# A fused deformable-convolution, attention and expert kernel: sums sent by ScalarE, values copied by VectorE, denser side work in the first 26 runs

## The chip, the cores and the metric

The kernel runs on one core of one Trainium2 chip. The metric is the device time of one execution in microseconds (us), the median of three runs.

## The reference

The input `x` has 4 images of 128 channels and 64 x 64 positions. All matrices are float32. Cut to what matters:

```python
# layer 0, for each image
xn  = group_norm(x)                           # 32 groups of 4 channels
om  = conv3x3(xn, w_off and w_mask)           # 18 offsets and 9 masks for every position
smp = bilinear(xn, at 9 taps moved by the offsets) * sigmoid(mask)
x   = x + einsum('bckhw,ock->bohw', smp, w) + bias

# layer 1, for each image: t has 4096 tokens of 128 values
def attn(v):                                  # v = layer_norm(t)
    h  = v.reshape(.., 16 heads, 8) + rx
    c  = cos(h); P = cumprod(c)
    q  = concat(prod(c[1:]), P[1:])           # 8 values per head: queries, keys and values at once
    s  = softmax(q @ q.T / sqrt(8))           # 4096 x 4096 scores per head
    x1 = layer_norm(v + (s @ q) @ w_comb.T)
    f  = relu(cos(x1[:, :8]) * cos(ry) @ w1.T) @ w2.T
    return layer_norm(x1 + f)
t = t + attn(layer_norm(t))
u = layer_norm(t)
p = softmax(u @ router)                       # 8 experts, the two best are taken
t = t + sum over the two best of p_e * (u @ expert_e)
```

## The kernel before, in words

An image is cut into 8 chunks of 512 positions, and its 16 heads into 4 groups of 4. Two kinds of work share the engines.

**Attention steps.** A run is one (image, head group, query chunk), and it goes over key tiles of 128 positions; each key tile is one step, 3700 steps in all. In a step TensorE makes the scores of four heads (`scores`, L1261, four matmuls into two PSUM tiles), ScalarE takes their exponential (L1270, two instructions of 128x1024), and TensorE adds values times exponentials to the run's sum `acc` (`context`, L1281). Scores run two steps ahead of the sums (`LAG`). Some exponentials of later stages are transposed (`turn`, L1140) and used again for the mirrored chunk pair (`from_turned`, L1214).

**Side work.** `prepare(b)` does layer 0 and the queries, keys and values of image `b`. For each chunk `deform` gathers the samples by GpSimd's indirect DMA (L625), weights and adds them on VectorE (L645 to L651), transposes them (L686), and sends them through memory (`smd`, L698 and L731). `convolved` multiplies them with the convolution's weights (`conv_ps`, 18 side products of four matmuls each, L281), adds bias and input on VectorE (L758), and goes on to `features`: layer norm, cosine and the running products `rn` (L822), the copy of `rn` into `fx` with a column of ones (L823, GpSimd), four DMAs of `fx` to `fqd` (L827), the transpose on TensorE (L836), its split into a high and a low part on VectorE (L838, L839), and eight DMAs of these into `kTd` and `qTd` (L846, L847). `finish(b, ch)` does the output projection, the feed-forward part (`feed_forward`) and the experts; up to two finishing jobs are open at once.

**What sets the order.** The order on TensorE, VectorE, SyncE and GpSimd is written out by a planner, class `Beside`. It keeps a clock `now` that moves on by 1.82 us a step, estimated ends of VectorE's and GpSimd's queues, and after each attention step it emits side work that fits. `fills` is how many pieces of side work with TensorE products it may emit in one step, `backlog` how many us of work may already be queued on VectorE. A DMA is put into the queue by `beside.later(when, emit)`, when the planner's clock gets to `when`. Each engine's queue is executed in its order.

**The first runs.** Image 0 has nothing to hide its layer 0 behind, so its attention starts with the chunks that are there. The first 26 runs (`opening`, 160 steps) work on chunks 0 to 3, in pieces; the names are `FIRST` for a run that starts a sum and `MORE` for one that goes on with a sum loaded from memory. Such a run of four steps loads the earlier sum (`cu<-part`, L1456), TensorE adds it through an identity matrix (`acc`, L281), ScalarE copies the total out of PSUM (L1491), and `park_sums` sends it back to memory over SyncE's queue (L1126). In later runs VectorE does the copy and nothing of this is on ScalarE.

The lines of the main loop that the change touches, before:

```python
beside.fills = 3 if run < 12 else 1
if streaming:                      # run < opening
    backlog = 1.5
...
if by_act:                         # run < opening
    nc.scalar.copy(cu, acc)
...
    park_sums(g, sc, cu, beside.now + 3.0 if by_act else beside.dve)
```

Of the kernel before, what the change touches and what calls it, by code (L numbers as in the profile page):

```python
# [22 lines left out]
P = 128  # L23
# [5 lines left out]
CH = 512  # L29
# [3 lines left out]
HD = 8  # L33
NGRP = 4
# [20 lines left out]
QG = 4 * QW  # L55
QL = QG
# [146 lines left out]
def need(pe=0.0, dve=0.0, lat=0.0, hold=False, after=0.0):  # L203

    return pe, dve, lat, hold, after


def ve(n, ops=1):  # L210

    return ops * (0.17 + n / 960.0)
# [6 lines left out]
def tr(n):  # L219

    return 0.13 + 0.115 * n
# [3 lines left out]
def kernel(  # L225
# [22 lines left out]
    nc = tc.nc  # L248
# [12 lines left out]
    beside = Beside()  # L261
# [156 lines left out]
    for i in range(NFX):  # L418
        t = big.tile([P, 4, QR], F32, name=f"fx{i}")
        nc.gpsimd.memset(t, 0.0)  # L420
        h = t[:, :, : HEADS * QW].rearrange("p j (h d) -> p j h d", d=QW)
# [9 lines left out]
    fqd = parked([NGRP, P, 4, QL], "fqd")  # L431
    kTd = parked([P * NGRP, CH], "kTd")
    qTd = parked([P * NGRP, CH], "qTd")
# [3 lines left out]
    partd = [[dram.tile([P, CH], F32, name=f"part{g}_{c}") for c in range(NCH)] for g in range(NGRP)]  # L437
# [355 lines left out]
    def features(b, ch, x2, mean, rstd):  # L793

        yield from layer_norm_stats(x2, mean, rstd, "lt")

        def temp(name, shape=(P, 4 * C), dt=F32):
            return work.tile(list(shape), dt, tag="p2", name=f"{name}{b}_{ch}", bufs=NP2)

        fx, f4 = fxs[ch % NFX]  # L800
        xt, a, n, r = temp("xt"), temp("ra"), temp("rn"), temp("rr")
        yield need(dve=ve(128, 4))
        normalized(xt.rearrange("p (i c) -> p i c", c=C), x2, mean, rstd)
        beside.later(
            beside.dve,
            lambda: nc.sync.dma_start(out=xtd[b][ch].rearrange("p i c -> p (i c)"), in_=xt),
        )
        yield need(dve=ve(512, 2))
        a8 = a.rearrange("p (h d) -> p h d", d=HD)
        x8 = xt.rearrange("p (h d) -> p h d", d=HD)  # L810
        nc.vector.tensor_tensor(a8, x8, rx_sb[:, None, :].to_broadcast([P, 64, HD]), ALU.add)
        yield from cosine(a, a, n, r, ve(512))
        c8 = a.rearrange("p (j h d) -> p j h d", j=4, d=HD)
        q8 = n.rearrange("p (j h d) -> p j h d", j=4, d=HD)
        yield need(dve=ve(64, 7))
        nc.vector.tensor_tensor(q8[:, :, :, 0], c8[:, :, :, 1], c8[:, :, :, 2], ALU.mult)
        for d in range(3, HD):
            nc.vector.tensor_tensor(q8[:, :, :, 0], q8[:, :, :, 0], c8[:, :, :, d], ALU.mult)
        yield need(dve=ve(64, 7), lat=0.2)
        nc.vector.tensor_tensor(q8[:, :, :, 1], c8[:, :, :, 0], c8[:, :, :, 1], ALU.mult)  # L820
        for d in range(2, HD):
            nc.vector.tensor_tensor(q8[:, :, :, d], q8[:, :, :, d - 1], c8[:, :, :, d], ALU.mult)  # L822
        beside.later(beside.dve, lambda: nc.gpsimd.tensor_copy(f4[:, :, :, :HD], q8))  # L823

        def put_values():
            for g in range(NGRP):
                nc.sync.dma_start(out=fqd[b % 2][ch][g], in_=fx[:, :, QG * g : QG * g + QL])  # L827

        beside.later(beside.dve + 2.0, put_values)

        yield need(pe=tr(4), dve=ve(512, 2))
        pt = misc(f"fT_ps{b}_{ch}")
        for i in range(4):
            nc.tensor.transpose(pt[:, P * i : P * (i + 1)], n[:, P * i : P * (i + 1)], ident)  # L836
        hi, lo = temp("hiT"), temp("loT")
        nc.vector.tensor_copy(hi.bitcast(F32R), pt)  # L838
        nc.vector.tensor_tensor(lo.bitcast(F32R), pt, hi, ALU.subtract)  # L839

        def put(part, fT):

            kd = kTd[b % 2][ch].rearrange("(h l r d) n -> l r h d n", l=2, r=2, d=HD)
            qd = qTd[b % 2][ch].rearrange("(h r l d) n -> l r h d n", l=2, r=2, d=HD)
            for rep in range(2):
                nc.sync.dma_start(out=kd[part, rep], in_=fT)  # L846
                nc.sync.dma_start(out=qd[part, rep], in_=fT)  # L847

        beside.later(beside.dve - ve(512), lambda: put(0, hi))
        beside.later(beside.dve, lambda: put(1, lo))  # L850
        prepared[b, ch] = beside.dve + 9.0
        featuring.pop(0)

# [65 lines left out]

    def feed_forward(b, ch, x4, a4):  # L920

        z3 = [
            work.tile([P, 4, HD], F32, tag=f"zf{k}", name=f"zf{k}{b}_{ch}") for k in range(3)
        ]
        zf = z3[0]
        yield need(dve=3 * ve(32))
        nc.vector.tensor_copy(zf, a4[:, :, :HD])
        yield from cosine(zf, *z3, ve(32))

        zx = work.tile([P, 4, 4, HD], F32, tag="zx", name=f"zx{b}_{ch}")  # L930
        yield need(dve=ve(32, 4), lat=0.2)
        nc.vector.tensor_tensor(zf, zf, cry[:, None, :].to_broadcast([P, 4, HD]), ALU.mult)
        nc.vector.tensor_copy(zx[:, :, 0, :].bitcast(F32R), zf)
        nc.vector.tensor_tensor(zx[:, :, 2, :].bitcast(F32R), zf, zx[:, :, 0, :], ALU.subtract)
        nc.vector.tensor_copy(zx[:, :, 1::2, :], zx[:, :, 0::2, :])
        yield need(pe=tr(4), dve=ve(512), lat=0.2)
        pz = misc(f"z_ps{b}_{ch}")
        for i in range(4):
            nc.tensor.transpose(
                pz[:32, P * i : P * (i + 1)], zx[:, i].rearrange("p l d -> p (l d)"), ident  # L940
            )
        zT = work.tile([32, 512], F32R, tag="f2", name=f"zT{b}_{ch}", bufs=NF2)
        nc.vector.tensor_copy(zT, pz[:32, :])
        hT = []
        for f in range(FFN // P):
            yield need(pe=0.43, dve=ve(512), lat=FREE if f < 3 else 0.2)
            ph = misc(f"h_ps{b}_{ch}_{f}")
            nc.tensor.matmul(ph, lhsT=w1_x[:, P * f : P * (f + 1)], rhs=zT, start=True, stop=True)  # L948
            h = temp2(f"h{b}_{ch}_{f}", (P, 512))
            nc.vector.tensor_scalar(h, ph, b1_sb[:, f : f + 1], 0.0, ALU.add, ALU.max)  # L950
            hT.append(h)
        yield need(dve=ve(512))
        nc.vector.tensor_tensor(a4, a4, bc4(b2), ALU.add)
        for i in range(4):
            for f in range(FFN // P):
                if f % 2 == 0:
                    last = i == 3 and f == 2
                    yield need(pe=2 * MM128, dve=ve(512) if last else 0.0, lat=0.0 if last else FREE, hold=not last)
                if i == 0 and f == 0:
                    pf = misc(f"f_ps{b}_{ch}")  # L960
                by_columns(
                    pf[:, C * i : C * (i + 1)], hT[f][:, P * i : P * (i + 1)], w2_sb[:, f, :],
                    f == 0, f == FFN // P - 1,
                )
        nc.vector.tensor_tensor(a4, a4, pf.rearrange("p (i c) -> p i c", c=C), ALU.add)  # L965
        m = work.tile([P, 4], F32, tag="ln_m", name=f"m2{b}_{ch}")
        rs = work.tile([P, 4], F32, tag="ln_r", name=f"r2{b}_{ch}")
        yield from layer_norm_stats(a4, m, rs, "ln")
        yield need(dve=ve(128, 4))
        normalized(a4, a4, m, rs)  # L970
        yield need(dve=ve(512, 2))
        nc.vector.tensor_tensor(a4, a4, bc4(g2), ALU.mult)
        nc.vector.tensor_tensor(a4, a4, bc4(beta2), ALU.add)
        yield need(dve=ve(512))
        nc.vector.tensor_tensor(x4, x4, a4, ALU.add)
# [144 lines left out]

        beside.later(beside.dve, put)

    def park_sums(g, sc, cu, when):

        def put():
            nc.sync.dma_start(out=partd[g][sc], in_=cu)  # L1126
            storing.discard((g, sc))

        storing.add((g, sc))
        beside.later(when, put)  # L1130

# [90 lines left out]

    landing = {}
    fetched = {}
    groups, done, active = {}, [], []

    def finishing():

# [179 lines left out]
    with tc.manual_schedule(engines={PE, DVE, SP, POOL}):  # L1410
# [6 lines left out]
        while n < len(steps):  # L1417
# [17 lines left out]
                    gives.remove(steps[m])  # L1435
                    turn(es[m - n], *steps[m])

            beside.fills = 3 if run < 12 else 1
            if streaming:
                backlog = 1.5  # L1440
            else:
                backlog = 0.4 if at >= len(ts) - 3 else 3.2
            if b + 1 < NB:
# [45 lines left out]
                cu = work.tile([P, 512], F32, tag="cu", name=f"cu{run}", bufs=NCU)  # L1489
            if by_act:  # L1490
                nc.scalar.copy(cu, acc)  # L1491
            elif kind in (WHOLE, FIRST):
                nc.vector.tensor_copy(cu, acc)  # L1493
            else:
                nc.vector.tensor_tensor(cu, cu, acc, ALU.add)
            if kind in (WHOLE, LAST):
                park_context(b, g, sc, cu)
            else:
                park_sums(g, sc, cu, beside.now + 3.0 if by_act else beside.dve)
        alone.append(True)  # L1500
        beside.drain()

# [72 lines left out]
```

## Time and profile before

| | |
|---|---|
| median of three runs | 7609.23 us (7607.39 to 7621.65) |
| profiled execution, its own time | 7579.71 us |
| its span, first to last instruction | 7576.5 us |
| mean granted TensorE clock | 0.968 |
| TensorE busy | 7113.9 us, 94% |
| ScalarE busy | 6863.5 us, 91% |
| VectorE busy | 4465.9 us, 59% |
| GpSimd busy | 1653.2 us, 22% |
| first exponential of step 0 | at 176 us |
| first exponential of step 160 (end of the first 26 runs) | at 637 us |
| last step's sums end | at 7493 us |

The share of TensorE is that of pipelined matmuls whose ends are modelled, so it reads high. SyncE and the DMA-issuing parts of the other engines are shown as queues (SPq, ACTq, POOLq): a row there is the time that the engine took to issue a transfer, not the transfer. In a list of waits a row names who waited, for whom, the sum in us, how many times, and the longest.

### The profile page before, as it was taken

The numbers are of one execution on the slowest core, as the hardware profiler recorded it, in microseconds if no ns is written. First come the engines' busy times: TensorE is split into PE (matmuls) and PEld (weight loads), VectorE is DVE, ScalarE is ACT, GpSimd is POOL, SyncE is SP. The second block draws the span as 40 slices with busy tenths as digits, with TensorE's granted clock in tenths as the row PEclk, the third lists the DMA queues.
The fourth block names the chain that finished last, engine by engine and source line by source line (L and its number), as shares of the span: only waits on it lengthen the run. The fifth ranks groups of instructions, "written<-read, shape, count | busy, mean of one in ns | idle before, by whom it ended". The sixth has DMA issues, their size and how long they took to land.

```text
span 7576.5 us, 180754 instructions
## 1 busy us (share of the span) xinstructions
PE 7113.9 (94%) x73848; PEld 2375.9 (31%) x73848; DVE 4465.9 (59%) x8950; ACT 6863.5 (91%) x7467; POOL 1653.2 (22%) x1326
## 2 busy tenths in 40 slices
PE   3688999899999999999999999999999999999997
PEld 2122222223333333333333323333333333333333
DVE  7755356667444877776544677775444554455434
ACT  0578999889999999999999998989999999999995
POOL 5544034443000433422000334431000000000000
PEclk6889999999999999999999999999999999999998
DMA  6777567978446878887655789897454466666661
GB/s 181 223 204 219 141 223 241 300 234 291 149 168 200 292 244 280 268 277 244 203 179 190 228 279 298 289 324 237 174 190 152 148 236 230 232 222 239 226 202 63
DMA packets 909788, 1689.51 MB, mean 223 GB/s; under 512 B 150754, under 2 KB 384124, under 8 KB 858268
## 3 DMA queue, kind: packets, MB, share of 16 engines
q1 hardware_dynamic: 809102, 1371.37, 54.9%
q0 software_dynamic: 92160, 302.06, 12.4%
q8 instruction: 579, 9.49, 0.5%
q10 hardware_dynamic: 7694, 4.52, 0.2%
q14 instruction: 253, 2.07, 0.1%
HBM read 1027.51 MB, written 650.14 MB: 221 GB/s over the span
## 4 chain that ended last, share of the span: by engine, by line
PE 80%; DMA 8%; DVE 4%; issue 2%; ACT 2%; SPq 1%; another core or an unknown queue 0%; POOL 0%; POOLq 0%; DVEq 0%; ACTq 0%
PE acc L1281 39%; PE sc L1261 24%; PE acc L1214 5%; PE e_ps L281 4%; PE conv_ps L281 3%; DMA et<-etd 2%; PE f_ps L281 2%; ACT e L1270 2%; DMA etd<-st 1%; DMA sT<-smd 1%; PE om_ps L533 1%; DMA smd<-tr 1%; DVE st L1140 1%; DVE v L645 1%; DMA cu<-part 1%
## 5 line engine op out<-in xcount | busy, mean ns | idle before, releaser
L1270 ACT ACTIVATE e<-sc 128x1024 f32<-128x1024 f32 x7400 | 6849.4, 1081 | 527.0 <-PE sc L1261 368.1
L1281 PE MATMUL acc<-e,qf 128*9 128x512 f32 (+1 forms) x29600 | 3938.3, 601 | 18.6 <-ACT cu L1491 7.5
L1261 PE MATMUL sc<-qT,kT 32*128 32x512 f32 x14800 | 2368.7, 499 | 153.3 <-ACT e L1270 84.8
L1261 PEld LDWEIGHTS sc<-qT,kT 32*128 32x128 f32 x14800 | 942.8, 183 | 3612.6 <-ACT e L1270 3130.4
L625 POOL DMA_INDIRECT v<-tab,idx x1152 | 1451.8, 1260 | 1579.3 <-DVE tr L686 956.2
L1140 DVE STREAM_TRANSPOSE st<-e 128x1024 f32<-128x1024 f32 x792 | 937.3, 1222 | 752.4 <-ACT e L1270 620.1
L1281 PEld LDWEIGHTS acc<-e,qf 128*9 128x9 f32 (+1 forms) x29600 | 682.4, 91 | 610.3 <-issue 346.8
L396 POOL TENSOR_TENSOR r<-ln_t,expo 128x4 f32<-128x4 f32 x96 | 112.2, 1169 | 3105.4 <-DVE ln_t L394 3057.0
L645 DVE TENSOR_TENSOR v<-v,wt 128x1536 f32<-128x1536 f32 x384 | 667.0, 1737 | 119.5 <-DMA v<-tab,idx 96.8
L1214 PE MATMUL acc<-et,qv 128*9 128x128 f32 x12672 | 506.4, 276 | 52.2 <-DMA et<-etd 44.6
L1065 DVE TENSOR_TENSOR eo<-e_ps,gt 128x512 f32<-128x512 f32 x256 | 175.2, 686 | 552.5 <-PE e_ps L281 547.5
L650 DVE TENSOR_TENSOR v<-v 128x768 f32<-128x768 f32 x384 | 367.2, 956 | 10.1
L281 PE MATMUL conv_ps<-sT,wconv_sb 128*32 128x256 f32 x4320 | 351.0, 399 | 15.7 <-DMA sT<-smd 11.6
L1214 PEld LDWEIGHTS acc<-et,qv 128*9 128x9 f32 x12672 | 270.0, 90 | 254.4 <-issue 212.6
L686 DVE STREAM_TRANSPOSE tr<-v 128x128 f32<-128x128 f32 x1080 | 249.4, 282 | 37.5 <-DMA etd<-st 28.7
L1493 DVE COPY cu<-acc 128x512 f32<-128x512 f32 x116 | 80.2, 692 | 306.3 <-PE acc L1281 260.8
L651 DVE TENSOR_TENSOR v<-v 128x384 f32<-128x384 f32 x384 | 215.7, 562 | 13.3
L396 POOL TENSOR_TENSOR rstd<-lt_t,expo 128x4 f32<-128x4 f32 x32 | 57.9, 1811 | 575.9 <-DVE lt_t L394 550.7
L281 PE MATMUL f_ps<-w_sb,h 128*32 128x128 f32 x4096 | 166.1, 282 | 0.1
L950 DVE TENSOR_SCALAR h<-h_ps,b_sb 128x512 f32<-128x512 f32 x128 | 94.9, 744 | 100.3 <-PE h_ps L948 89.9
L823 POOL COPY fx<-rn 128x512 f32<-128x512 f32 x32 | 26.8, 838 | 526.3 <-DVE rn L822 321.4
L965 DVE TENSOR_TENSOR a<-a,f_ps 128x512 f32<-128x512 f32 x32 | 21.9, 685 | 198.8 <-PE f_ps L281 198.8
(227 smaller groups left out, 3166.9 us busy)
## 6 DMA issues: line engine op xcount, KB each, us to landing
etd<-st SPq DMA_DIRECT2D x396, 1024.0 KB
et<-etd SPq DMA_DIRECT2D x396, 1024.0 KB
kT<-kTd SPq DMA_DIRECT2D x372, 256.0 KB
smd<-tr SPq DMA_DIRECT2D x360, 192.0 KB
sT<-smd SPq DMA_DIRECT2D x360, 192.0 KB
qT<-qTd SPq DMA_DIRECT2D x166, 256.0 KB
atd<-cu SPq DMA_DIRECT2D x128, 256.0 KB
qf<-fqd SPq DMA_DIRECT2D x372, 72.0 KB
```

The lines of the kernel that those rows point to most:

```text
L281: nc.tensor.matmul(dst[c : c + 32], lhsT=lhsT[:, c : c + 32], rhs=rhs, start=start, stop=stop)
L625: nc.gpsimd.indirect_dma_start(out=v[:, k, :], out_offset=None, in_=tab, in_offset=bass.IndirectOffsetOnAxis(ap=idx[:, j, kk : kk + 1], ax ...
L645: nc.vector.tensor_tensor(v4, v4, w12[:, :, None].to_broadcast([P, 12, C]), ALU.mult)
L650: nc.vector.tensor_tensor(v[:, :, : 2 * C], v[:, :, : 2 * C], v[:, :, 2 * C :], ALU.add)
L651: nc.vector.tensor_tensor(v[:, :, :C], v[:, :, :C], v[:, :, C : 2 * C], ALU.add)
L686: nc.vector.transpose(out=tr9[:, k, :, j % 4, :], in_=v[:, k, :C].rearrange("p (c i) -> p c i", i=32),)
L1065: nc.vector.tensor_tensor(ws[hf], pe.rearrange("p (e c) -> p e c", c=C), gt[:, i, 4 * hf : 4 * (hf + 1), None].to_broadcast([P, 4, C]), AL ...
L1140: nc.vector.transpose(out=st[:, :, 2 * pr : 2 * pr + 2, :].rearrange("p o h (q j) -> p o (h q) j", j=32), in_=es[pr].rearrange("p h (q o i ...
L1214: nc.tensor.matmul(acc[32 * h : 32 * h + QW, P * kt : P * (kt + 1)], lhsT=qv[:, at : at + QW], rhs=e[:, :, h, 32 * t : 32 * (t + 1)], star ...
L1261: nc.tensor.matmul(ps[i // 2][:, i % 2, :], lhsT=kT[h : h + 32, P * (t % 4) : P * (t % 4 + 1)], rhs=qT[h : h + 32, :], start=True, stop=True,)
L1270: nc.scalar.activation(e, ps[pr], AF.Exp, scale=1.0 / math.sqrt(HD))
L1281: nc.tensor.matmul(acc[32 * h : 32 * h + width, :], lhsT=flat[:, first : first + width], rhs=es[h // 2][:, h % 2, :], start=(t == ts[0]), ...
```

## The change

It does six things.

1. In the first 26 runs, in place of the first 12, up to three pieces of side work with TensorE products are emitted in a step.
2. In these runs VectorE's queue may hold 4.0 us in place of 1.5 us.
3. In these runs ScalarE issues the store of its sum itself, in its own queue.
4. `rn` is copied into `fx` by VectorE, after the high and the low part, and `fx` is sent by one DMA in place of four, last.
5. `hiT` and `loT` are sent by two DMAs each in place of four; a row of the tile is written twice by a repeated source, and the order of rows within a head becomes (d, part, repeat) in keys and (d, repeat, part) in queries.
6. `feed_forward` waits while another finishing job is inside its feed-forward part (list `heavy`).

```diff
@@ features
-        beside.later(beside.dve, lambda: nc.gpsimd.tensor_copy(f4[:, :, :, :HD], q8))
-        def put_values():
-            for g in range(NGRP):
-                nc.sync.dma_start(out=fqd[b % 2][ch][g], in_=fx[:, :, QG * g : QG * g + QL])
-        beside.later(beside.dve + 2.0, put_values)
-        yield need(pe=tr(4), dve=ve(512, 2))
+        yield need(pe=tr(4), dve=ve(512, 3))
...
         nc.vector.tensor_tensor(lo.bitcast(F32R), pt, hi, ALU.subtract)
+        nc.vector.tensor_copy(f4[:, :, :, :HD], q8)
         def put(part, fT):
-            kd = kTd[b % 2][ch].rearrange("(h l r d) n -> l r h d n", l=2, r=2, d=HD)
-            qd = qTd[b % 2][ch].rearrange("(h r l d) n -> l r h d n", l=2, r=2, d=HD)
-            for rep in range(2):
-                nc.sync.dma_start(out=kd[part, rep], in_=fT)
-                nc.sync.dma_start(out=qd[part, rep], in_=fT)
-        beside.later(beside.dve - ve(512), lambda: put(0, hi))
-        beside.later(beside.dve, lambda: put(1, lo))
+            kd = kTd[b % 2][ch].rearrange("(p l r) n -> l p r n", l=2, r=2)
+            qd = qTd[b % 2][ch].rearrange("(p r l) n -> l p r n", l=2, r=2)
+            twice = fT[:, None, :].to_broadcast([P, 2, CH])
+            nc.sync.dma_start(out=kd[part], in_=twice)
+            nc.sync.dma_start(out=qd[part], in_=twice)
+        def put_values():
+            nc.sync.dma_start(
+                out=fqd[b % 2][ch].rearrange("g p t x -> p t g x"),
+                in_=fx.rearrange("p t (g x) -> p t g x", g=NGRP),
+            )
+        beside.later(beside.dve - 2.0 * ve(512), lambda: put(0, hi))
+        beside.later(beside.dve - ve(512), lambda: put(1, lo))
+        beside.later(beside.dve, put_values)
@@ feed_forward
+        while heavy:
+            yield need(lat=1.0)
+        heavy.append(True)
...
         nc.vector.tensor_tensor(a4, a4, pf.rearrange("p (i c) -> p i c", c=C), ALU.add)
+        heavy.pop()
@@ main loop
-            beside.fills = 3 if run < 12 else 1
+            beside.fills = 3 if streaming else 1
             if streaming:
-                backlog = 1.5
+                backlog = 4.0
...
             if by_act:
                 nc.scalar.copy(cu, acc)
+                nc.scalar.dma_start(out=partd[g][sc], in_=cu)
...
-            else:
-                park_sums(g, sc, cu, beside.now + 3.0 if by_act else beside.dve)
+            elif not by_act:
+                park_sums(g, sc, cu)
```

More of the change, by code (lines that the diff above doesn't have):

```diff
@@ L1121, in park_context, with park_sums @@
         beside.later(beside.dve, put)
-    def park_sums(g, sc, cu, when):
+    def park_sums(g, sc, cu):
         def put():
@@ L1129, in park_sums @@
         storing.add((g, sc))
-        beside.later(when, put)
+        beside.later(beside.dve, put)
     def turn(es, run, t):
@@ L1226 @@
     fetched = {}
-    groups, done, active = {}, [], []
+    groups, done, active, heavy = {}, [], [], []
     def finishing():
```

## The prediction

> **What bounds the kernel now.** I read the page first, then busy time by stage.
>
> ```profile
> PE 7113.9 (94%) x73848; PEld 2375.9 (31%) x73848; DVE 4465.9 (59%) x8950; ACT 6863.5 (91%) x7467; POOL 1653.2 (22%) x1326
> 176.00:640.00 464.00, 349.01 (x2756) 101.16 (x2752) 306.57 (x556) 315.19 (x349) 250.12 (x190) 0.84 0.74 225
> 640.00:1000.00 360.00, 341.78 (x2812) 99.77 (x2812) 154.17 (x304) 335.13 (x364) 69.68 (x56) 0.97 0.52 150
> 1000.00:5300.00 4300.00, 4141.34 (x42659) 1358.67 (x42647) 2780.92 (x5304) 4021.37 (x4360) 1184.61 (x947) 0.98 0.76 247
> 5300.00:7493.00 2193.00, 2190.35 (x24672) 758.23 (x24674) 1049.36 (x2437) 2189.67 (x2394) 52.28 (x51) 1.00 0.58 199
> ```
>
> The columns are length, then busy us of PE, PEld, DVE, ACT, POOL, then granted clock. In the last long stage ScalarE idles 3 us of 2193: its exponentials set the pace: 2394 of them in 2193 us, two a step, so 1.83 us a step. TensorE fits beside them as long as a step carries one side product. So the time is 3700 steps at that pace plus ScalarE's idle time: 176 us ahead of the first step, 149 us in the first 26 runs (176 to 640), 25 us to 1000, 279 us to 5300, and the 84 us tail. Five of the six edits aim at the second term. The gaps there, from ScalarE's timeline:
>
> ```profile
> 267.53 5.61 ACT L1270 ACTIVATE e<-sc 128x1024 f32<-128x1024 f32 x6 [45.60 <-PE sc L1261]
> 286.54 0.59 ACT L1491 COPY cu<-acc 128x512 f32<-128x512 f32 x1 [10.68 <-issue]
> 491.94 5.61 ACT L1270 ACTIVATE e<-sc 128x1024 f32<-128x1024 f32 x6 [14.00 <-PE sc L1261]
> 509.71 0.58 ACT L1491 COPY cu<-acc 128x512 f32<-128x512 f32 x1 [9.43 <-PE acc L281]
> 900.73 3.77 ACT L1270 ACTIVATE e<-sc 128x1024 f32<-128x1024 f32 x4 [10.83 <-PE sc L1261]
> ```
>
> 267 is the wait for chunk 1, 492 for the keys of chunk 3, 900 for those of chunk 7. The gaps before copies (L1491) are runs whose earlier sum came late from memory; those of 0.3 us and more add up to 42 us (10.7, 4.2, 0.3, 2.2, 9.4, 1.8, 2.0, 4.1, 7.4). Then the waits from 0 to 760 us, SyncE's queue among them:
>
> ```profile
> SPq L1126 <- ACT cu L1491: 113.8, 15, 19.9
> SPq L827 <- POOL fx L823: 45.0, 6, 13.4
> DVE xr L758 <- PE conv_ps L281: 88.7, 5, 25.6
> PE sc L1261 <- DMA kT<-kTd: 37.2, 3, 22.0
> ```
>
> SyncE's queue, which carries nearly every transfer, stands 114 us behind stores that wait for ScalarE and 45 us behind GpSimd's copy; VectorE stands 89 us waiting for convolutions that are fed one product a step.
>
> **The change part by part**, against the profiled 7579.7 us (span 7576.5 and 3.2 around it); the median of the runs shown is 7609.2, 29.5 above. Signs: minus is a gain.
>
> *Key and value path (edits 4, 5).* For chunk 0 SyncE issues fqd from 153.26 to 155.86, and the eight stores of high and low parts from 156.41 to 162.81, about 0.6 us each; the loads start at 170.39 when these have landed. With four stores in place of eight, and fqd behind them, the keys' last store goes out up to 4 us earlier. Each new store is twice as big, so its issue may take 0.6 us as now or twice that: the gain is between 0 and 4. I take 4, as the issue of fqd's four quarters shows no growth with more and smaller pieces (0.65 each). For chunk 1 fqd runs from 244.78 and kTd's last from 253.21, with smd's stores behind; four issues less and fqd gone from the front are about 5 us of the 45.6. Together −9 (0 to −14). The copy on VectorE costs 0.43 us (its cheapest 512-wide pass, L373) to 0.69 us (L811), 32 times, 14 to 22 us. I take 0.69, since it writes rows of 9. VectorE is 59% busy and the copy stands behind the high and low parts, so nothing waits for it but fqd: 0; uncovered it costs 22. GpSimd's queue loses 32 copies that stand in front of gathers: from 441.6 to 458.3 no gather was issued, because the copy waited for `rn`.
>
> A rule speaks against this edit. The Trainium skill, SBUF — State Buffer, section SBUF: two separate sides, says that an fp32 copy from SBUF to SBUF on VectorE locks GpSimd out of descriptor generation, so that gathers stall. By that rule the 32 copies would each hold the gathers up for their length, at most 22 us in all, 5.5 us of it in the eight of image 0. In this case's trace the gathers' issues take 0.94 to 2.4 us each beside a busy VectorE, and this spread may hold such holds already; one more pass of 0.69 us in a chunk of 36 gathers and some 75 us of VectorE work is below what I count.
>
> *Three side products a step (edit 1) and the longer queue (2).* The built instruction lists of the changed kernel have the convolution of chunk 3 in steps 68 to 73 in place of 70 to 87, and the transposes L836 of chunks 2 to 7 at steps 45, 88, 126, 165, 230, 278 in place of 47, 100, 136, 186, 237, 282. Chunk 3's keys are first needed at step 104, now 16 steps (29 us) after the transpose and not 4: the wait of 14.0 goes, −14 (what is next there is the sum of the next row). Chunk 7 is needed from step 288 on; 4 steps earlier (7.3 us) and a shorter put take 9 of the 10.8. What it costs is seen where image 0 already ran three a step:
>
> ```profile
> 303.38 1.94 ACT L1270 ACTIVATE e<-sc 128x1024 f32<-128x1024 f32 x2 [0.27 <-PE sc L1261]
> 306.10 1.94 ACT L1270 ACTIVATE e<-sc 128x1024 f32<-128x1024 f32 x2 [0.79 <-PE sc L1261]
> 308.84 1.94 ACT L1270 ACTIVATE e<-sc 128x1024 f32<-128x1024 f32 x2 [0.80 <-PE sc L1261]
> ```
>
> A step with three products takes 2.73 us, one with a single product 1.86 (TensorE's sums at 416.99, 418.86 and 420.72). Three convolutions (chunks 3, 4, 5), 18 triple steps: 18 x 0.87 = 15.7, less the 36 steps that lose their product, 36 x 0.03 = 1.1: +14.6. Where the run waits for its sum anyway it is hidden; bounds +5 and +15, I take +14. The longer queue puts up to 2.5 us more of gathers' sums ahead of a convolution's result on VectorE; behind that wait TensorE's single side bank. I take 0 (−5 to +10).
>
> *Sums by ScalarE (3).* 26 stores leave SyncE. Each costs ScalarE an issue: ACTq rows of like size took 0.36 to 0.44 us, so 26 x 0.40 = 10.4; ScalarE is busy 315 of 464 there, and busier at run ends: +8 (bounds 7 and 11). What SyncE gains is the place of the next loads. A load of a sum still stands behind `sT` and `smd` issues, and behind the store two runs before it, which uses the same buffer. So I take a third of the 42 us, −14 (0 to −42). There is a new wait: in the built lists each DMA of SyncE and ScalarE takes the next of eight completion counters and waits until the previous DMA on that counter has landed. So ScalarE, with all later exponentials queued behind it, waits for a transfer of SyncE eight DMAs back. For 17 of the 26 that was emitted 6 steps or more (11 us) before. Nine are nearer; the worst is the store of run 24, in the same step as a `sT` load. Loads here took 6.5 to 13 us: +8 (0 to +40, if SyncE runs late for a dozen of them).
>
> The Trainium skill, DMA: Bandwidth & Descriptors, section Issuing engines are not separate DMA queues, says that spreading DMAs over issuing engines saves sequencer issue time alone. By that the gain would be 26 x 0.33 = 8.6 us of SPq's issue, and not more; the row of 113.8 us says that the queue's wait is worth more than its issue.
>
> *One job in the feed-forward part (6).* The lists have the same TensorE work left after step 3700, so the tail stays at 84. Jobs interleave otherwise; the side work done by step 2000 is 1% less. Of the 279 us of gaps to 5300, many are `et<-etd` landing late or scores waiting for exponentials, which a new interleaving shifts either way. I take 0, bounds −20 and +20.
>
> Sum: −9 −14 −9 +14 +8 −14 +8 = −16. GpSimd's queue, whose gathers start up to 16 us earlier in a chunk, should now and then free VectorE: −3 (0 to −10). That is −19: 7560.7 for a profiled execution like this one, about 7590 against the median of 7609.2.
>
> **Rivals.** *The queue was the whole trouble.* All waits for sums go, chunk 7's whole wait too, and ScalarE's new wait is nothing: −9 −14 −11 +14 +8 −42 = −54, 7555. For it: 114 us on one row. Against: sums late at 388.79 and 496.30 were issued right behind `sT` loads, which stay.
>
> *ScalarE is tied to SyncE (slower).* ScalarE, the pacing engine, inherits SyncE's lateness through the eight counters. If a dozen stores wait 6.5 us (the landing at 277.61 to 284.5), it is 78 us; with the first sum without its +8 (−24) the result is +54, 7663; with eight such waits +28, 7637. It decides from 24 us on, four such waits. For it: SyncE's stores of `smd` wait for VectorE, whose queue is now longer. Against: the planner's step is 1.82 us and real steps of this stage take 2.9, so SyncE is rather ahead of the list than behind.
>
> *Given back.* The chunks come earlier than any step needs (chunks 4 and 5 are needed at step 256 only), and triple steps cost what the waits gave: 7609.
>
> **How the numbers follow.** Own sum 0.45, whole queue 0.20, tied to SyncE 0.25, given back 0.10. A measurement tells 0.2% (15 us) from no change. My own sum lies just beyond that, its bounds on both sides of it: 0.25 faster, 0.15 same, 0.05 slower. The whole queue is faster, 0.20. Tied: 0.22 slower, 0.03 same. Given back: 0.06 same, 0.04 slower. Total 0.45, 0.24, 0.31. The range from 7540 to 7645 takes in the second rival's time and the first half of the third's; the likeliest case alone, whose bounds are not all met at once, is 7570 to 7615.
>
> **What would show it.** Right: step 160 begins some 20 us earlier than 637; no gap of 14 us at chunk 3; the row SPq for ScalarE's copy gone; triple steps of 2.7 us in runs 13 to 25. Wrong: ScalarE's queue waiting several us before its stores; gaps at copies as long as before; or a difference that arises after 1000 us, where I count nothing.

## The result, and the profile after

The changed kernel takes **7678.2 us** (median of four runs, 7667.1 to 7685.5) against 7608.3 for the kernel before in the same comparison: ratio **1.0089 [1.0068, 1.011]**, some 70 us slower. The forecast was 7590, range 7540 to 7645, most likely a gain. The profiled execution of the changed kernel takes 7684.0 us, 6 above its median; that of before lies 29 under its own. The two traces are therefore 104 us apart, the medians 70, and I use the traces for where the loss arises rather than for its size.

The first line is from the page; the others are busy time by stage, with the columns of the prediction (the stages begin at the same steps as there, to within some us):

```profile
PE 7144.8 (93%) x73848; PEld 2383.3 (31%) x73848; DVE 4473.2 (58%) x8982; ACT 6866.5 (89%) x7467; POOL 1620.4 (21%) x1294
```

```profile
180.00:634.00 454.00, 353.10 (x2808) 104.66 (x2808) 313.49 (x594) 316.10 (x351) 233.82 (x179) 0.87 0.77 227
634.00:1000.00 366.00, 349.33 (x2816) 101.31 (x2820) 147.56 (x275) 341.75 (x371) 71.14 (x58) 0.96 0.53 151
1000.00:5400.00 4400.00, 4154.23 (x42417) 1357.04 (x42411) 2775.72 (x5290) 4010.05 (x4344) 1164.21 (x922) 0.97 0.74 241
5400.00:7600.00 2200.00, 2196.56 (x24859) 762.43 (x24860) 1060.59 (x2475) 2196.31 (x2401) 52.78 (x52) 1.00 0.58 198
```

ScalarE's busy time is what it was; its idle time grew. It idles 138 us in the first stage (149 before) and 390 us in the third, which is 4400 us long (279 in 4300 before). The fourth is still limited by the exponentials, with 4 us idle. The start of a step's first exponential in both traces says where:

| step | before, us | after, us | difference |
|---|---|---|---|
| 104 | 491.9 | 486.3 | -5.7 |
| 160 | 637.0 | 629.9 | -7.1 |
| 288 | 882.3 | 871.8 | -10.6 |
| 400 | 1108.5 | 1101.8 | -6.7 |
| 800 | 1940.0 | 1957.6 | +17.6 |
| 1200 | 2702.5 | 2732.9 | +30.4 |
| 1720 | 3725.4 | 3793.5 | +68.1 |
| 2500 | 5276.7 | 5383.6 | +106.9 |
| 3699 | 7489.9 | 7596.6 | +106.8 |

The first image gains 11 us. Steps 400 to 2500, in which images 1 to 3 are prepared beside the scores, lose 114 us. After that nothing changes. This is the third of the signs that the prediction named as proof against itself: a difference where it counted nothing.

**The opening.** From ScalarE's timeline (start, duration, operation, idle time ahead of it and what ended it):

```profile
269.92 5.61 ACT L1275 ACTIVATE e<-sc 128x1024 f32<-128x1024 f32 x6 [41.68 <-PE sc L1266]
291.19 0.59 ACT L1496 COPY cu<-acc 128x512 f32<-128x512 f32 x1 [12.93 <-PE acc L281]
490.34 1.23 ACT L1275 ACTIVATE e<-sc 128x1024 f32<-128x1024 f32 x1
490.67 0.33 ACTq L1497 DMA_DIRECT2D part<-cu  x1
498.40 0.59 ACT L1496 COPY cu<-acc 128x512 f32<-128x512 f32 x1 [4.08 <-PE acc L281]
589.63 0.59 ACT L1496 COPY cu<-acc 128x512 f32<-128x512 f32 x1 [14.94 <-PE acc L281]
886.88 1.94 ACT L1275 ACTIVATE e<-sc 128x1024 f32<-128x1024 f32 x2 [7.44 <-PE sc L1266]
```

The 14.0 us wait for chunk 3's keys is gone: around 490 the exponentials run through. Steps 70 to 72, with three products each, take 2.66 to 2.79 us, near the 2.73 forecast; where loads came late, others took up to 4.4. The wait for chunk 7 is 7.4 in place of 10.8. But the gaps ahead of copies, most of which end with a sum's load, are not smaller: all rows with a gap add up to 58 us, to 49 before (the 42 of the prediction leave out four rows of 0.3 us and more). ScalarE's own store (ACTq) starts 0.03 us after the copy's end in 25 of 26 cases, 0.27 in the other: no long wait for a completion counter shows.

The wait for chunk 1 is 4 us shorter only because the first step began 3.7 us later (at 179.9, before at 176.2). From the start of VectorE's pass `hiT`, which makes the chunk's keys, to the first exponential on them it took 20.1 us before (247.46 to 267.53) and takes 24.5 now (245.38 to 269.92). SyncE's queue shows where, first before, then after:

```profile
254.79 4.12 SPq L698 DMA_DIRECT2D smd<-tr  x4
261.00 0.34 SPq L1239 DMA_DIRECT2D kT<-kTd  x1
```

```profile
249.70 1.67 SPq L844 DMA_DIRECT2D fqd<-fx  x1
251.46 11.82 SPq L698 DMA_DIRECT2D smd<-tr  x4
263.78 0.41 SPq L1244 DMA_DIRECT2D kT<-kTd  x1
```

The keys' last store is issued 5 us earlier than before. But the four stores of samples (`smd`) behind the value transfer now take 11.8 us to issue, and the loads of the keys stand behind them.

**The middle.** What TensorE and the scores waited for between 900 and 5400 us (sum in us, times, longest):

```profile
ACT e L1275 <- PE sc L1266: 235.6, 146, 13.0
PE acc L1219 <- DMA et<-etd: 64.8, 20, 10.2
PE conv_ps L281 <- DMA sT<-smd: 41.1, 8, 11.6
```

The same three rows of before read 154.9, 44.6 and 7.8. ScalarE waits 81 us more for scores, and TensorE waits 54 us more for loads: of samples (`sT`) for the convolutions, and of turned exponentials (`et`). Both are issued by SyncE. The granted clock of the third stage is 0.97, before 0.98, and TensorE is busy 4154 us in it, before 4141; whether the lower clock adds to the gaps or follows from them isn't shown.

### The profile page after: what moved, and what is told of

It is laid out like the page before. It is cut to its first block, busy times and chain, and to the rows that moved or that the text cites. A ratio compares the mean times of both kernels' runs of the same rounds, so it can differ in the third digit from the quotient of the medians.

```text
span 7682.2 us, 180344 instructions
## 1 busy us (share of the span) xinstructions
PE 7144.8 (93%) x73848; PEld 2383.3 (31%) x73848; DVE 4473.2 (58%) x8982; ACT 6866.5 (89%) x7467; POOL 1620.4 (21%) x1294
## 4 chain that ended last, share of the span: by engine, by line
PE 81%; DMA 8%; DVE 3%; issue 3%; SPq 2%; ACT 2%; POOL 1%; another core or an unknown queue 0%; ACTq 0%; POOLq 0%; DVEq 0%
PE acc L1286 39%; PE sc L1266 24%; PE acc L1219 5%; PE conv_ps L281 4%; PE e_ps L281 3%; DMA et<-etd 3%; DMA sT<-smd 2%; ACT e L1275 2%; PE f_ps L281 2%; PE om_ps L533 1%; DMA a<-rdd 1%; POOL v L625 1%; SPq L722 1%; PE ao_ps L281 1%
## 5 line engine op out<-in xcount | busy, mean ns | idle before, releaser
L281 PEld LDWEIGHTS conv_ps<-sT,wconv_sb 128*32 128x32 f32 x4320 | 92.1, 110 | 184.6 <-issue 163.3
L758 DVE SCALAR_TENSOR_TENSOR xr<-conv_ps,bconv_sb,xr 128x128 f32<-128x128 f32 x128 | 35.9, 343 | 153.3 <-PE conv_ps L281 144.9
```

The source lines that it names most:

```text
L281: nc.tensor.matmul(dst[c : c + 32], lhsT=lhsT[:, c : c + 32], rhs=rhs, start=start, stop=stop)
```

## The experiments

Each group of runs shares one chip and the runs of the kernel before on it. Chips differ (the unedited kernel takes 7463 to 7614 us), so only ratios and differences within a group are compared; where a trace is laid against that of before across groups, it says so. The planner's step, `STEP`, is a constant of 1.82 us by which it places side work. Another value changes no operation, only the step in which each is emitted; I call that re-dealing.

**Which edit loses? (7611.1 before)** Parts of the change alone, as hunks of the diff above.

```diff
open_only:      edits 1, 2, 3     lock_only:     edit 6
open_and_lock:  edits 1, 2, 3, 6  path_and_lock: edits 4, 5, 6
```

> The kernel before with edits 1, 2 and 3 alone (the first 26 runs); value path and feed-forward part as before. The two traces differ by 11 us in favour of the change up to step 300 and by 118 us against it from step 400 to step 2500, so the loss should not be here. Queue theory (the value path's transfers, edits 4 and 5, block SyncE's queue): 7595, some 11 us faster than before, and no loss after step 400. Lock theory (edit 6 makes the loss): the same 7595. Re-dealing theory (any edit shifts the planner's order in images 1 to 3, and a new order costs tens of us whoever made it): 7590 to 7670, with a loss after step 400, since this edit too shifts the later order.

> The kernel before with edit 6 alone: one finishing job at a time in its feed-forward part. Lock theory: 7670 to 7700, nearly the whole loss, between steps 800 and 2500, where the finishing jobs run. Queue theory: 7600 to 7615, no loss. Re-dealing theory: anywhere from 7580 to 7660.

> The changed kernel without edits 4 and 5: edits 1, 2, 3 and 6, with GpSimd's copy of the values, four value transfers ahead of eight key and query stores. Queue theory: the loss is gone, 7590 to 7605. Lock theory: the loss stays, 7665 to 7690. Re-dealing theory: between the two, with no relation to the sum of the single parts.

> The kernel before with edits 4, 5 and 6, the first 26 runs as before. Queue theory: 7680 to 7700, the whole loss without the gain of the opening, and the transfer that follows the single value transfer takes several us to issue in every chunk, as in the changed kernel. Lock theory: the same time as with the lock alone. Re-dealing theory: anywhere from 7590 to 7690.

Measured: open_only 7606.6, 0.9995 [0.9985, 1.0005]; lock_only 7637.8, 1.004 [1.0025, 1.0054]; open_and_lock 7645.8, 1.0049 [1.0033, 1.0066]; path_and_lock 7665.1, 1.0072 [1.0055, 1.0089]. Laid against the first trace of before (another run, of nearly the same time), step 300 comes 10 us earlier in open_only, and by step 500 the gain is gone. So the opening edits do what the traces of the whole change showed, and give nothing in the end. The lock alone seems to cost 27 us. Without edits 4 and 5 (open_and_lock) half the loss is there, which neither the queue theory nor the lock theory had forecast. Edits 4 and 5 without edit 6 were not tried.

**Is it the lock, the form of the path, or the order? (7578.5 before)** The lock could cost by what it does, or only because any new order does.

```diff
old_path_same_order: changed kernel, with GpSimd's copy, four fqd DMAs
                     ahead of the transpose, eight stores
small_transfers:     changed kernel, with four fqd DMAs last, eight stores
redealt_before:      before, and
-    STEP = 1.82
+    STEP = 1.81
redealt_lock:        before with edit 6, and
-    STEP = 1.82
+    STEP = 1.83
```

> The changed kernel with the old value and key path (GpSimd's copy, four value transfers ahead of eight stores), but with the planner told what it is told in the changed kernel. TensorE and ScalarE execute exactly the changed kernel's order, VectorE too but for the copy; only the transfers' form and place differ. Queue theory: the path's share comes back, 7640 to 7655, since the transfer behind the single value transfer no longer takes 5 us to issue. Re-dealing theory: it stays at 7670 to 7685, since the order is that of the changed kernel.

> The changed kernel with four value transfers and eight stores again in their old forms, but in the changed kernel's places (high, low, values last) and with VectorE's copy. All orders but SyncE's are those of the changed kernel. Queue theory, form: 7640 to 7655, the burst of 256-row transfers is what blocks the queue. Queue theory, place: 7670 to 7685, the same pieces in the same place fill the queue whoever cuts them, and the next transfer still takes several us. Re-dealing theory: 7670 to 7685.

> The kernel before with nothing changed but the planner's idea of a step, 1.81 us in place of 1.82. The work and all mechanisms are the same; the order of side work is dealt anew. Re-dealing theory: the time moves by 20 us or more, up or down. Lock and queue theories: 7600 to 7620, as before.

> The kernel with edit 6 alone (7638 against 7611 in the run before), and the planner's step at 1.83 us in place of 1.82. Lock theory: 7630 to 7650, the lock costs the same in any order. Re-dealing theory: it moves by 15 us or more from 7638, either way.

Measured: old_path_same_order 7657.4, 1.0094 [1.0077, 1.0111]; small_transfers 7678.7, 1.0127 [1.0109, 1.0146]; redealt_before 7602.2, 1.0025 [1.0015, 1.0035]; redealt_lock 7554.1, **0.9953 [0.9935, 0.9972]** (its medians alone give 0.9968). The first of these is the plainest: with the old value and key path back, in the changed kernel's order, the loss is as large as that of the whole change. The queue theory had forecast that some half of it would go, the re-dealing theory that all of it would stay. In the trace of old_path_same_order, steps 300 to 2500 take 4449 us, in that of before (another chip) 4360, in the changed kernel's 4478:

```profile
912.70:5361.70 4449.00, 4218.15 (x43103) 1379.99 (x43104) 2781.91 (x5278) 4082.14 (x4420) 1188.05 (x954) 0.98 0.74 240
```

ScalarE idles 367 us there, before 283. The lock theory falls too: with the lock and a planner step 0.01 us longer the kernel is faster than either version (it has the lowest ratio found). And 0.01 us of planner step alone moves the unedited kernel by 0.25%. Smaller transfers do not help while they stand last, so the size of a single transfer is not the cause.

**How far does re-dealing move the changed kernel? (7602.0 before)**

```diff
changed_again: as changed      changed_183: changed, STEP = 1.83
changed_181: changed, STEP = 1.81
open_and_lock_183: edits 1, 2, 3, 6, STEP = 1.83
```

> The changed kernel itself, so that its re-dealt forms are compared on one chip: 1.009 times before, as found.

> The changed kernel with all six edits and the planner's step at 1.83 us in place of 1.82: same work, same mechanisms, side work dealt anew. Re-dealing theory: it moves by 20 us or more from the changed kernel, and downwards, since the changed kernel's order is the worst of those seen: a ratio to before of 0.995 to 1.006. Queue and lock theories: 1.006 to 1.012, as the changed kernel.

> The same with 1.81 us. Re-dealing theory: a ratio between 0.995 and 1.008, not that of the other two. Queue and lock theories: 1.006 to 1.012.

> Edits 1, 2, 3 and 6 with the planner's step at 1.83 us. The lock with 1.83 gave 0.9953 of before. If the opening's 10 to 15 us came on top: 0.993 to 0.994. Re-dealing theory: the edits of the opening shift the order again, so no such sum holds: 0.994 to 1.006.

Measured: changed_again 7663.7, 1.0078 [1.0061, 1.0095]; changed_183 7661.9, 1.0073 [1.0046, 1.0101]; changed_181 7626.8, 1.0034 [1.0019, 1.0048]; open_and_lock_183 7638.9, 1.0056 [1.0038, 1.0074]. The loss repeats on another chip. Re-dealing takes some 37 us of it away, but none of the three orders tried of the changed kernel gets back to the time before. That points to something besides the order, but three orders do not show it.

**The place of the value transfers (7614.2 before).** The same instruction order on TensorE and ScalarE in both of the first two kernels; the copy is VectorE's and the transfers are the small ones in both. Only the place differs: `fqd` ahead of the transpose, as before the change, or last, behind `loT`.

```diff
 place_values_last = small_transfers; place_values_first:
+        nc.vector.tensor_copy(f4[:, :, :, :HD], q8)
+        def put_values(): ...    # four DMAs
+        beside.later(beside.dve + 2.0, put_values)
         yield need(pe=tr(4), dve=ve(512, 3))
...
-        beside.later(beside.dve, put_values)
 lock_184: edit 6, STEP = 1.84     before_180: before, STEP = 1.80
```

> The changed kernel's order on TensorE, ScalarE and GpSimd, VectorE's copy, four value transfers and eight stores, but the values' copy and transfers ahead of the transpose as in the kernel before. Against the same pieces with the values last (next run): if the place is what costs, some 20 us less, as with the old path; if GpSimd's copy was what helped there, no difference.

> The same pieces with the values last (small_transfers again, as the partner of the run above on one chip). Place: some 20 us above it. No place: equal within 8 us. Either way 1.007 to 1.013 of before.

> Edit 6 alone with the planner's step at 1.84 us. With 1.82 it was 1.004 of before, with 1.83 it was 0.995. If the lock itself costs some 30 us and 1.83 was a lucky order: 1.002 to 1.006. If the order alone decides: anywhere from 0.995 to 1.005.

> The kernel before, without any edit, with the planner's step at 1.80 us. 1.81 gave 1.0025. If orders without the lock are better as a family: 0.998 to 1.003. If the order alone decides: anywhere from 0.995 to 1.006.

Measured: place_values_first 7659.3, 1.0052 [1.0036, 1.0069]; place_values_last 7730.8, 1.0145 [1.0128, 1.0162]. The place alone is worth 72 us, far more than the 20 expected. lock_184 takes 7633.9, 1.0025 [1.0011, 1.0038], which both theories allow. before_180 takes 7672.9, 1.007 [1.0053, 1.0088], above what both allow: a version of the unedited kernel loses nearly as much as the change.

**The same with one transfer (7462.6 before).** The whole change, and the whole change with only its `fqd` DMA and the copy in front of it moved back ahead of the transpose.

```diff
 changed_control: as changed; changed_values_first:
+        nc.vector.tensor_copy(f4[:, :, :, :HD], q8)
+        def put_values(): ...    # the one DMA of the change
+        beside.later(beside.dve + 2.0, put_values)
         yield need(pe=tr(4), dve=ve(512, 3))
...
-        beside.later(beside.dve, put_values)
```

> The changed kernel, transfers in its own forms and VectorE's copy, with the copy and the one value transfer back in their old place, ahead of the transpose and of the eight... now four stores. All other orders are the changed kernel's. If the place costs in this form too: 20 us or more below the changed kernel (next run), 1.003 to 1.006 of before, and the transfer behind the burst no longer takes 5 us to issue. If only the cut into four with values last is bad: equal to the changed kernel, 1.008 to 1.009.

> The changed kernel as it is, on the same chip: 1.008 to 1.009 of before.

Measured: changed_values_first 7457.6, **0.9992 [0.9983, 1.0001]**; changed_control 7523.7, **1.0082 [1.0068, 1.0096]**. That is 66 us, as much as the change had lost on this chip (61). Between the two traces the difference is +1 us at step 300, +25 at 800, +49 at 1720 and +63 from 2500 on. It arises in the same stretch as the loss of the change. Steps 300 to 2500 of each, in the columns used above, control first:

```profile
889.60:5219.80 4330.20, 4136.33 (x43105) 1359.14 (x43107) 2787.44 (x5302) 4070.96 (x4421) 1183.09 (x930) 0.98 0.75 247
```

```profile
888.20:5156.50 4268.30, 4123.51 (x43101) 1357.02 (x43102) 2789.59 (x5304) 4069.66 (x4420) 1182.71 (x930) 0.98 0.76 251
```

The same work, with the clock at 0.98 in both; TensorE is busy 13 us longer in the control. ScalarE idles 259 us in one and 199 in the other, and this is 61 of the 62 us. One of the places, around step 465: first SyncE's queue and TensorE in changed_control,

```profile
1188.66 1.25 SPq L841 DMA_DIRECT2D qTd<-loT  x1
1190.01 1.28 SPq L844 DMA_DIRECT2D fqd<-fx  x1
1191.34 3.17 SPq L1461 DMA_DIRECT2D cu<-part  x1
...
1195.99 8.93 SPq L731 DMA_DIRECT2D sT<-smd  x8
1207.21 0.93 PE L1266 MATMUL sc<-qT,kT 32*128 32x512 f32 x4
1213.09 1.08 PE L281 MATMUL conv_ps<-sT,wconv_sb 128*32 128x256 f32 x8 [4.95 <-DMA sT<-smd]
```

and then the same place in changed_values_first:

```profile
1181.65 0.62 SPq L826 DMA_DIRECT2D fqd<-fx  x1
...
1187.33 1.25 SPq L847 DMA_DIRECT2D qTd<-loT  x1
1188.63 1.31 SPq L1460 DMA_DIRECT2D cu<-part  x1
...
1192.29 4.83 SPq L731 DMA_DIRECT2D sT<-smd  x8
1205.55 0.92 PE L1265 MATMUL sc<-qT,kT 32*128 32x512 f32 x4
1206.40 0.64 PE L281 MATMUL conv_ps<-sT,wconv_sb 128*32 128x256 f32 x8
```

Here the values go out 4 us ahead of the first of the keys' stores (1185.5), in a pause of the queue. In the control they stand between the keys' stores and the next chunk's loads. There the DMA behind them takes 3.17 us to issue in place of 1.31, the eight `sT` loads are issued by 1204.9 in place of 1197.1, and the first convolution of the next chunk waits 4.95 us. TensorE's queue, with all the scores, stands behind it. The five steps from 465 take 15.9 us in the control and 9.4 in the other. At steps 530, 575, 1405 and 2150, too, the control falls behind by 5 to 8 us within ten steps. The longest waits there are 9.5 us for `et` (1405, in the other kernel 2.8) and 13.5 and 9.3 us for `sT` (575 and 2150, in the other 9.0 and 3.7), not all of them directly behind a value transfer. From 900 to 5250 us TensorE's waits for `sT` add up to 47.1 us against 25.8, those for `et` to 91.8 against 76.9: 36 of the 62 us are on these two rows.

**Five forms in one order.** These kernels have the same order on TensorE and ScalarE. They ran on several chips, so differences between rows, other than those of the two pairs above, are estimates; the one form that ran twice here, four transfers last, differs by 0.0018 (14 us) between its two chips.

| kernel | copy | value transfers | key and query stores | ratio to before |
|---|---|---|---|---|
| old_path_same_order | GpSimd | four, first | eight | 1.0094 |
| place_values_first | VectorE | four, first | eight | 1.0052 |
| small_transfers, place_values_last | VectorE | four, last | eight | 1.0127, 1.0145 |
| changed_values_first | VectorE | one, first | four | 0.9992 |
| changed (three chips) | VectorE | one, last | four | 1.0078 to 1.0089 |

So the new order costs some 0.9% with the path as it was. VectorE's copy and the fewer transfers give back about as much (some 32 and 46 us) while the values go first. Putting the values last takes 66 us of that away again. The place was tested in this one order only; what it is worth in another isn't shown.

## Why the prediction was wrong

**The step that failed: "I take 0, bounds −20 and +20" for a new interleaving.** The prediction knew that jobs would interleave otherwise, and that 279 us of gaps lay where this acts, and put the term at nothing. It did so for edit 6 alone, though every edit that the planner sees deals the side work anew: open_only, without edit 6, is 10 us ahead at step 300 and behind at step 500. In the changed kernel's order, with the value and key path of before, the time is 1.0094 of before (old_path_same_order): some 71 us, the size of the whole loss, and in the same steps, 300 to 2500. The bounds were not worked out from any row. A planner step moved by 0.01 or 0.02 us, with no edit at all, costs 0.25 and 0.7% (redealt_before, before_180); edit 6 alone gives 1.004, 0.9953 and 1.0025 in three orders, so no cost of its own can be told from this. The spread of all these is 1.2%, some 90 us. Why one order is better than another stays open.

**The second: the place of `fqd`, in the key and value path.** Here "four issues less and fqd gone from the front are about 5 us" counts what the move frees for the keys. The text names `smd`'s stores behind, but puts nothing on what the queue carries next. SyncE works its list in order, and behind a chunk's last DMA stand the loads of the next one. Even for chunk 1, the row that the prediction reasoned from, the sign was wrong: from `hiT` to the first exponential it takes 4.5 us longer, and with the values first (changed_values_first, on another chip) 17.7 us, 2.4 less than before. In images 1 to 3 nothing was counted, and there the place costs most of its 66 us (changed_values_first against changed_control), 72 us in the small form.

**The term of the whole path, −9, came out by luck.** In the same order, the path of the change stands at 1.0078 to 1.0089 and the old one at 1.0094: 4 to 12 us less, from different chips, and not told from nothing by their intervals. Behind this stand two larger numbers that the prediction did not have: some 78 us of gain from VectorE's copy and the fewer transfers, and 66 us of loss from the place.

How the place turns into a delay is shown in part. In the one-transfer form, the issue directly behind `fqd` takes 2.1 us or more in all but the first chunk: in the changed kernel 162 us in 32 chunks, median 3.8, against 27 us, median 0.37, in changed_values_first, where the same DMA goes first. In the small form that issue takes 0.87 us in the median (place_values_last), and the place costs as much. So the long issue is not the cause by itself. What both forms share is that the value pieces, 2048 of 144 bytes in a chunk, are in the DMA queues ahead of the next loads. At the place shown above, around step 465, the packets show what that does. In the control, from 1193.2 to 1195.5 us:

```profile
DMA packets 2126, 0.39 MB, mean 169 GB/s; under 512 B 2080, under 2 KB 2080, under 8 KB 2126
...
q1 hardware_dynamic: 2126, 0.39, 93.7%
```

For these 2.3 us the 16 DMA engines are 94% busy with the value pieces, and only 46 larger packets run. In changed_values_first the same pieces run from 1182.9 to 1184.9, before the keys' stores are issued. How much of the 66 us arises in this way over all chunks was not measured.

**The opening was right in its mechanism, too large in its sum.** Chunk 3's wait went (-14 forecast), the triple steps took about what was forecast, and chunk 7's wait shrank by 3.4 us (-9 forecast). "A third of the 42 us, -14" for the sums failed: the gaps before copies grew from 49 to 58 us. Loads of sums still stand behind other transfers of SyncE, as the argument against the first rival had said. ScalarE's feared wait (+8) measured nothing. "Step 160 begins some 20 us earlier" measured 7.1. The Trainium skill, DMA: Bandwidth & Descriptors, section Issuing engines are not separate DMA queues, would give the 26 stores 8.6 us (the prediction's estimate, 26 x 0.33) and no more; open_only, with an interval of -11 to +4 us for three edits together, cannot tell that from nothing.

**Terms that held.** VectorE's copy hides, at 0.42 us rather than the 0.69 taken; 32 of them are 14 us beside an engine that is 58% busy. The Trainium skill's rule (SBUF — State Buffer, section SBUF: two separate sides) that such a copy locks GpSimd out of descriptor generation shows no cost here: of the seven gathers' issues that overlap such a copy in the changed kernel, the longest took 1.05 us, where the median of all 1152 is 0.96. And place_values_first, with VectorE's copy, loses less than old_path_same_order with GpSimd's, though on another chip. The tail is 82 us (84 forecast).

**The rivals.** ScalarE tied to SyncE named 7663, close to the result, by a mechanism that did not occur: its stores did not wait (0.03 us behind the copy) and the loss is not in the opening. *The queue was the whole trouble* fell with the gaps before copies. *Given back* describes open_only, and changed_values_first in the end, but not the change.

## What to carry to other kernels

When a transfer is moved in an in-order queue, list what stands behind its new place in every stage, not only what waits for the transfer itself; here a store whose reader comes late cost 66 us by its place ahead of loads that TensorE waits for. Where a planner decides the order, re-deal it by one constant before predicting: the spread seen there (1.2% here) belongs into the bounds of any edit that changes the order, and a smaller effect needs two kernels with the same order.

## What the runs showed of the hardware

- An issue on SyncE right behind one DMA of 2048 pieces of 144 bytes took 2.1 to 12.9 us in 31 of 32 chunks of the changed kernel (median 3.8), where that DMA itself stood behind the chunk's four stores of keys and queries, 0.5 MB each. Where it went ahead of those stores, the issue behind it took 0.37 us in the median (changed_values_first); split into four DMAs, at the last place, 0.87 (place_values_last).
- A DMA of such pieces, 0.29 MB, kept the 16 DMA engines over 90% busy for 2.0 us (changed_values_first, 1182.9 to 1184.9), at 147 GB/s; the stores of 2048-byte pieces ran at 353 GB/s (changed_control, 1190 to 1193).
- A copy of 128x512 on VectorE between two tiles took 0.42 us, also where it writes rows of 9 (shortest, median and longest in ns):

```profile
L833 DVE COPY fx<-rn x32: 416/417/672, 160.0 to 5350.4; 128x512 f32<-128x512 f32 x32
```

- The unedited kernel took 7463 us on the fastest of four chips and 7614 on the slowest, 2% apart.
